# Normalizing half the rows ahead of the other half's additions at the ends of two graph layers

## The chip, the core and the metric

The kernel runs on one core of one Trainium2 chip. The metric is the time of one execution in device microseconds; the time before is the median of 6 runs. A core has five engines with a queue of instructions each: PE (TensorE, matrix products; its weight loads are listed apart as PEld), DVE (VectorE), ACT (ScalarE), POOL (GpSimd) and SP (SyncE, which here issues transfers). Each engine takes its instructions strictly in the order in which they were built; a wait for another engine holds everything behind it on the same engine. Products land in PSUM and are copied out by DVE or ACT (an evacuation); everything else lies in SBUF, 128 partitions wide, or in DRAM.

## The reference

Four graph layers run one after the other on 2708 nodes with 128 features and one dense adjacency matrix `adj`, each followed by a residual addition and a layer norm:

```
x = layernorm(x + L0(x, adj))   # messages gelu(s_i + d_j + b), summed with weights adj_ij; update with gelu, inner layernorm
x = layernorm(x + L1(x, adj))   # gated messages, see below; update with relu, inner layernorm
x = layernorm(x + L2(x, adj))   # a hyperbolic layer over all pairs
x = layernorm(x + L3(x, adj))   # two rounds of adj @ x with swish
```

Layer 1, whose start and end the change touches:

```
messages = x @ W_msg + b_msg
logits = (messages @ W_q) @ (messages @ W_k).T / sqrt(128) + gate_bias
gates = sigmoid(logits) * adj * adj
updated = relu(concat([x, gates @ messages]) @ W_upd + b_upd)
out = (updated - mean) / sqrt(var + eps) * gamma + beta
```

So at the end of layers 0 and 1 each row is normalized twice: first the layer's own result `h`, which is scaled by gamma and added to x + beta, and then the sum. The second result is the x of the next layer.

## The kernel before, in words

**Tiles.** x is held as 22 tiles of 128 rows (the last has 20). `groups()` gives groups of 4 tiles, `runs()` two halves: tiles 0 to 10 (early) and 11 to 21 (late).

**The two normalizations.** `moments` (L197) takes one bn_stats per tile on DVE. `normalize` (L199 to L230) works out the scale `r` and the offset `off` of every row of a half in some ten small DVE instructions of 128x11 (L129, L150, L205) with one square root on ACT between them (L145), and then shifts each tile: even tiles on DVE (L230), odd ones on ACT (L228). `Resnorm.add(a, b)` normalizes `h`, multiplies it by gamma (L241), adds it to `xb`, which is x + beta (L242), and takes the moments of the sum. `Resnorm.end(a, b)` normalizes x itself. `Resnorm.all` runs add of the early half, add of the late half, end of the early half, end of the late half.

**End of layer 0.** It is written in the order in which it shall run (`manual_schedule`). `U.sums(n)` forms the update of a group on PE (L821), adds it on DVE (L822) and applies Gelu on ACT (L823); `U.rows(n)` adds x (L828), takes moments and adds beta to x on POOL (L830). After five groups `U.norm.add` runs for the early half; then come the sums and rows of the last two tiles, then the late half and both ends. After that stand the five small DVE instructions of the bad count (L899 to L904; a count of rows for which the sparse method of layer 0 would not hold), a 1x1 product on PE (L906), and a copy of it to `bad_n` (L907), which is read before layer 3.

**Start of layer 1.** A scheduler places these instructions by their operands. PE turns W_q and W_k (L1007), multiplies them to `w_qk` (L1012); then, for each group, x is turned (L1019) and copied to `xT` on ACT (L1020), `ps_m` (L1022) gives the messages, copied to mT on ACT (L1023), `ps_q` (L1025) the queries, copied to qT on DVE (L1026), and `ps_w` (L1031) gives messages and the x part of the update side by side, which DVE copies to `both` with a bias (L1032). For that, POOL first copies two weights and two biases into `w_both` and `b_both` (L1001, L1002). POOL also forms `xb` (L1034). In the main loop `lg` (L1063), a sigmoid (L1064), two multiplications by the adjacency tile (L1065, L1066) and `acc` (L1070) run for each tile; SyncE loads the adjacency tiles (L1054) into three buffers.

**End of layer 1 and start of layer 2.** `norm.all()` closes layer 1, in written order. Then, placed by the scheduler: x is turned (L259), copied to another `xT` on DVE and ACT in turn (L261), multiplied by the layer 2 weights (L1176), copied to `M` on ACT (L1177), and DVE takes its moments (L1179) before a long chain of small instructions.

Of the kernel before, what the change touches and what calls it, by code (L numbers as in the profile page):

```python
# [12 lines left out]
F32 = mybir.dt.float32  # L13
# [3 lines left out]
ALU = mybir.AluOpType  # L17
# [3 lines left out]
P = 128  # L21
BANK = 512
# [12 lines left out]
def spans(start, stop, step):  # L35
    return [(a, min(a + step, stop)) for a in range(start, stop, step)]
# [3 lines left out]
def gnn_stack(ctx: ExitStack, tc: tile.TileContext, t, out: bass.AP):  # L40
    nc = tc.nc
    N, D = t["x"].shape
# [6 lines left out]
    const = ctx.enter_context(tc.tile_pool(name="const", bufs=1))  # L49
# [5 lines left out]
    @functools.cache  # L55
    def weight(name, k0=0):
        w = const.tile([P, D], F32, name=f"w_{name}_{k0}")
        nc.sync.dma_start(out=w, in_=t[name][k0:k0 + P, :])
        return w

    @functools.cache
    def column(name):
        c = const.tile([P, 1], F32, name=f"col_{name}")
        nc.sync.dma_start(out=c, in_=t[name].rearrange("(p o) -> p o", o=1))
        return c

    @functools.cache
    def across(name):
        n = t[name].shape[0]
        r = const.tile([P, n], F32, name=f"row_{name}")  # L70
        nc.gpsimd.dma_start(out=r, in_=t[name].partition_broadcast(P))
        return r


    x = keep.tile([P, NT, D], F32, name="x")
    xsq = keep.tile([P, NT], F32, name="xsq")
    bad_n = keep.tile([1, 1], mybir.dt.int32, name="bad_n")
# [13 lines left out]
    def over_tiles(r, n=NT, p=P):  # L91
        return r[:p, None, :].to_broadcast([p, n, r.shape[1]])
# [8 lines left out]
    class Values:  # L101
# [33 lines left out]
        def add(self, a, b):  # L135
            return self.tt(a, b, ALU.add)
# [53 lines left out]
    def runs(n=2):  # L190

        return [(NT * k // n, NT * (k + 1) // n) for k in range(n)]

    def moments(st, src, a, b):

        for i in range(a, b):
            nc.vector.bn_stats(out=st[:, i, :], in_=src[:, i, :])  # L197

    def normalize(dst, src, st, a, b, V, sq=None):  # L199

        even, odd, m2, m5 = (st[:, a:b, k] for k in (1, 4, 2, 5))

        def stt(in0, scalar, in1, op0, op1):
            o = V.new(in0)
            nc.vector.scalar_tensor_tensor(o, in0, scalar, in1, op0=op0, op1=op1)  # L205
            return o


        d = V.tt(even, odd, ALU.subtract)
        q = stt(d, 1.0 / 16.0, d, ALU.mult, ALU.mult)  # L210
        if sq is None:
            m = stt(m2, LN_EPS * D, m5, ALU.add, ALU.add)
            w = stt(m, 0.25 / D, q, ALU.mult, ALU.add)
        else:
            m = V.tt(m2, m5, ALU.add)
            var = stt(m, 0.25 / D, q, ALU.mult, ALU.add)
            w = V.ts(var, 0.25 * LN_EPS, ALU.add)

        root = V.act(w, AF.Sqrt)
        both = V.tt(even, odd, ALU.add)  # L220
        r = V.recip(V.add(root, V.mul(w, V.recip(root))))
        off = stt(both, -0.5, r, ALU.mult, ALU.mult)
        if sq is not None:
            nc.vector.scalar_tensor_tensor(sq[:, a:b], var, 4.0 * D, V.mul(r, r), op0=ALU.mult, op1=ALU.mult)
        for i in range(a, b):
            c = slice(i - a, i - a + 1)
            if i % 2:
                nc.scalar.activation(dst[:, i, :], src[:, i, :], AF.Identity, bias=off[:, c], scale=r[:, c])  # L228
            else:
                nc.vector.tensor_scalar(dst[:, i, :], src[:, i, :], r[:, c], off[:, c], op0=ALU.mult, op1=ALU.add)  # L230

    class Resnorm:


        def __init__(self, h, xb, g, st, st2, V, sq=None):
            self.h, self.xb, self.g, self.st, self.st2, self.V, self.sq = h, xb, g, st, st2, V, sq

        def add(self, a, b):
            h = self.h
            normalize(h, h, self.st, a, b, self.V)  # L240
            nc.vector.tensor_tensor(h[:, a:b, :], h[:, a:b, :], over_tiles(self.g, b - a), op=ALU.mult)  # L241
            nc.vector.tensor_tensor(x[:, a:b, :], self.xb[:, a:b, :], h[:, a:b, :], op=ALU.add)  # L242
            moments(self.st2, x, a, b)

        def end(self, a, b):
            normalize(x, x, self.st2, a, b, self.V, self.sq)

        def all(self):
            for a, b in runs():
                self.add(a, b)  # L250
            for a, b in runs():
                self.end(a, b)

    def transposed(dst, src, psum):

# [121 lines left out]
    with ExitStack() as l0:  # L377
        wp = l0.enter_context(tc.tile_pool(name="l0", bufs=1))
        aggT = wp.tile([P, LT * LR], F32, name="aggT")
        msg_s, msg_d = weight("L0_msg_wT", 0), weight("L0_msg_wT", P)  # L380
        upd_x, upd_a = weight("L0_upd_wT", 0), weight("L0_upd_wT", P)
        msg_b, msg_br = column("L0_gnn_msg_b"), across("L0_gnn_msg_b")
        upd_b, ln_w, ln_b = across("L0_gnn_upd_b"), across("L0_gnn_ln_w"), across("L0_gnn_ln_b")
# [4 lines left out]
        with ExitStack() as msg:  # L388
# [37 lines left out]
            with tc.tile_pool(name="pre0", bufs=1) as pp:  # L426
# [3 lines left out]
                    out=trif[:, :JB], in_=trif[:, :JB], compare_op=ALU.is_gt, fill=0.0, base=0,  # L430
# [23 lines left out]
            p_misc = msg.enter_context(tc.tile_pool(name="ps_misc", bufs=1, space=PSUM))  # L454
# [378 lines left out]
            U = Update()  # L833
# [4 lines left out]
            with tc.manual_schedule():  # L838
# [43 lines left out]
                for step in last_turn:  # L882
                    step()
                U.rows(ahead - 1)
                early, late = runs()
                U.norm.add(*early)
                for n in range(ahead, G):
                    U.sums(n)
                for n in range(ahead, G):
                    U.rows(n)  # L890
                U.norm.add(*late)
                U.norm.end(*early)
                U.norm.end(*late)


                most = vp.tile([P, 1], F32, name="most")
                ones = vp.tile([P, 1], F32, name="ones")
# [4 lines left out]
                nc.vector.tensor_tensor(bad, bad, fine, op=ALU.subtract)  # L902
                nc.vector.tensor_scalar(bad, bad, 1.0, None, op0=ALU.add)
                nc.vector.tensor_reduce(most, bad, AX.X, ALU.add)  # L904
                ps = p_misc.tile([P, BANK // P, P], F32, name="ps")
                nc.tensor.matmul(ps[:1, 0, :1], ones, most, start=True, stop=True)  # L906
                nc.vector.tensor_copy(bad_n, ps[:1, 0, :1])  # L907

    def all_pairs():

# [65 lines left out]
    def layers_1_to_3(top, before_end=lambda: None):  # L976

        with ExitStack() as l1:
# [6 lines left out]

            both = wp.tile([P, NT, 2 * D], F32, name="both")
            mrow, h = both[:, :, :D], both[:, :, D:]
            w_both = wp.tile([P, 2 * D], F32, name="w_both")
            b_both = wp.tile([P, 2 * D], F32, name="b_both")
            xb = wp.tile([P, NT, D], F32, name="xb")  # L990
            w_msg, w_q, w_k = weight("L1_gnn_W_msg"), weight("L1_gnn_W_q"), weight("L1_gnn_W_k")
            upd_x, upd_a = weight("L1_gnn_W_upd", 0), weight("L1_gnn_W_upd", P)
            msg_bc, msg_br = column("L1_gnn_b_msg"), across("L1_gnn_b_msg")
            gate_b = across("L1_gnn_gate_bias")
            upd_b, gamma, beta = across("L1_gnn_b_upd"), across("L1_gnn_ln_gamma"), across("L1_gnn_ln_beta")

            with ExitStack() as pre:
                psum = pre.enter_context(tc.tile_pool(name="ps_pre1", bufs=2, space=PSUM))
                nc.gpsimd.memset(both[:, NT - 1, :], 0.0)
                for k, (w, b) in enumerate(((w_msg, msg_br), (upd_x, upd_b))):  # L1000
                    nc.gpsimd.tensor_copy(w_both[:, k * D:(k + 1) * D], w)  # L1001
                    nc.gpsimd.tensor_copy(b_both[:, k * D:(k + 1) * D], b)  # L1002

                wT = []
                for w in (w_q, w_k):
# [120 lines left out]
        with ExitStack() as l2:  # L1126
            wp = small
# [565 lines left out]
```

## Time and profile before

| what | value |
|---|---|
| median of 6 runs | 1961.28 us (1960.13 to 1963.07) |
| profiled execution | 1956.19 us |
| its span, first to last instruction | 1954.5 us |
| mean granted clock of TensorE | 0.924 |
| busy share of the span: PE, DVE, ACT, POOL | 84%, 79%, 57%, 35% |
| end of layer 0, from the last far sums' stage to the bad count's product | 879 to 927 us |
| start of layer 1 up to the first gate product | 927 to 954.89 us |
| end of layer 1 and start of layer 2 | 1172 to 1208 us |

Start times are us from the span's start. A group or a piece of the chain is named by engine, what is written, and line. "busy, mean" of an instruction is its own time; the step to a dependent instruction behind it is a little longer, and independent instructions of DVE overlap a little. The chain that ended last is followed back from the last instruction: at each step to what released it, or to the instruction before it on its engine. Queue waits (SPq) tell what a queue's next transfer waited for.

### The profile page before, as it was taken

To read this page: it belongs to the slowest core of one execution; us is meant where nothing else is said; L and a number is where in the kernel's file an instruction comes from. 1 tells how busy PE (TensorE), PEld (TensorE's weight loads), DVE (VectorE), ACT (ScalarE), POOL (GpSimd) and SP (SyncE) were. 2 spreads that over 40 slices of the span, in tenths; PEclk is the share of its full clock that TensorE was granted. 3 is DMA by queue.
4 is the path that set the end of the run, shared out by engine and by line. 5 is a ranking of instruction groups with operands and counts; after the bars stand their busy time and mean duration, and the time that the engine had idled before them with its cause. 6 is when DMAs were issued, how large, how long until landed. Compare 5 with 4: busy or idle time off the path is not lost.

```text
span 1954.5 us, 36493 instructions
## 1 busy us (share of the span) xinstructions
PE 1650.5 (84%) x13993; PEld 945.9 (48%) x13993; DVE 1549.0 (79%) x3657; ACT 1118.9 (57%) x1551; POOL 677.1 (35%) x431
## 2 busy tenths in 40 slices
PE   5999999999999999881999992899889972099995
PEld 4666666666666666661544441322223321044542
DVE  7899999999999999868688858699999997800104
ACT  3666676676676666653344434799989973300003
POOL 5677667667767767571100000020000440000000
PEclk9899999999999999995999996789999986599997
DMA  8756656666666566440344401122223207044320
GB/s 224 156 118 144 140 124 146 131 130 147 127 131 150 122 136 141 81 89 5 138 150 165 151 2 59 45 89 88 74 69 101 92 2 299 0 166 151 138 94 30
DMA packets 218695, 222.25 MB, mean 114 GB/s; under 512 B 28373, under 2 KB 204859, under 8 KB 212051
## 3 DMA queue, kind: packets, MB, share of 16 engines
q1 hardware_dynamic: 167470, 196.15, 32.5%
q0 software_dynamic: 51040, 23.68, 10.3%
q8 instruction: 111, 1.82, 0.4%
q14 instruction: 74, 0.60, 0.1%
HBM read 211.94 MB, written 7.83 MB: 112 GB/s over the span
## 4 chain that ended last, share of the span: by engine, by line
DVE 42%; PE 30%; POOL 8%; issue 7%; ACT 6%; DMA 6%; SPq 0%; DVEq 0%; ACTq 0%; POOLq 0%
PE acc L1604 10%; POOL far L739 7%; PE lg L1063 5%; PE acc L1070 5%; DVE ix L735 5%; DMA far<-d_tab,ix 4%; DVE W L840 3%; DVE w L1336 3%; DVE u L1322 3%; DVE m L1325 3%; DVE extra L753 2%; DVE o L697 2%; DVE S L665 2%; DVE m L1342 2%; PE sl L775 2%
## 5 line engine op out<-in xcount | busy, mean ns | idle before, releaser
L739 POOL DMA_INDIRECT far<-d_tab,ix x352 | 561.1, 1594 | 259.9 <-DVE W L840 112.5
L853 ACT ACTIVATE g<-sl 128x768 f32<-128x768 f32 x484 | 392.9, 812 | 257.9 <-PE sl L780 204.8
L775 PE MATMUL sl<-dA,S 124*128 124x153 f16 x4840 | 408.0, 231 | 10.4 <-DVE W L840 7.6
L775 PEld LDWEIGHTS <-S 124*128 124x128 f16 x4840 | 330.3, 98 | 79.9 <-issue 68.1
L791 PE MATMUL acc<-g,W 128*32 128x128 f32 x4840 | 205.5, 277 | 0.5 <-DVE W L840 0.5
L1296 POOL TENSOR_TENSOR at<-at,off 128x128 f32<-128x128 f32 (+1 forms) x22 | 69.4, 3167 | 337.6 <-DMA at<-in_adjT 322.4
L1604 PE MATMUL acc<-held,x 128*128 128x512 f32 (+1 forms) x240 | 99.7, 564 | 82.6 <-ACT x L228 82.6
L791 PEld LDWEIGHTS acc<-g,W 128*32 128x32 f32 x4840 | 140.6, 109 | 58.7 <-issue 54.8
L780 PE MATMUL sl<-s,same 50*128 50x384 f16 x968 | 161.8, 308 | 0.0
L280 DVE TENSOR_TENSOR g<-ps,row_L_gnn_b 128x512 f32<-128x512 f32 (+2 forms) x14 | 7.9, 573 | 191.7 <-PE ps L278 191.6
L1352 PE MATMUL accV<-m,X 128*128 128x512 f32 (+4 forms) x264 | 128.3, 628 | 33.8 <-DVE m L1342 29.4
L840 DVE TENSOR_TENSOR W<-sl,own 128x150 f32<-128x150 f32 x484 | 143.0, 299 | 14.8 <-ACT g L853 12.1
L1304 PE MATMUL ps<-XT 128*128 128x512 f32 (+4 forms) x264 | 143.1, 626 | 3.1 <-ACT m L1309 2.8
L1064 ACT ACTIVATE w<-lg,row_L_gnn_gate_bias 128x512 f32<-128x512 f32 (+1 forms) x132 | 83.4, 636 | 106.1 <-PE lg L1063 104.9
L665 DVE TENSOR_SCALAR S<-rk 124x1000 f16<-124x1000 bf16 (+1 forms) x330 | 132.8, 428 | 0.0
L735 DVE FIND_INDEX8 ix<-v,o 128x8 uint32<-128x2728 f32 x44 | 131.7, 2993 | 0.0
L1063 PE MATMUL lg<-qT,mT 128*128 128x512 f32 (+2 forms) x264 | 121.1, 547 | 3.6 <-ACT w L1064 3.1
L1070 PE MATMUL acc<-w,both 128*128 128x512 f32 (+2 forms) x264 | 121.2, 546 | 0.0
L753 DVE SCALAR_TENSOR_TENSOR extra<-far,v,extra 128x128 f32<-128x128 f32 x330 | 114.7, 348 | 6.3
L1604 PE MATMUL acc<-at,x 128*128 128x512 f32 (+3 forms) x288 | 118.4, 559 | 0.0
L697 DVE SCALAR_TENSOR_TENSOR o<-ps,ar 128x496 f32<-128x496 f32 x132 | 82.4, 624 | 37.5 <-issue 24.5
L1604 PEld LDWEIGHTS acc<-held,x 128*128 128x128 f32 x240 | 45.1, 197 | 134.8 <-ACT x L228 82.8
(315 smaller groups left out, 2618.8 us busy)
## 6 DMA issues: line engine op xcount, KB each, us to landing
at<-in_adjT SPq DMA_DIRECT2D x40, 1354.0 KB
ar<-in_adj SPq DMA_DIRECT2D x105, 248.0 KB
far<-s_tab SPq DMA_DIRECT2D x44, 512.0 KB
at<-in_adjT SPq DMA_DIRECT2D x42, 448.0 KB
at<-in_adjT SPq DMA_DIRECT2D x21, 704.0 KB
at<-in_adjT SPq DMA_DIRECT2D x21, 650.0 KB
held<-in_adjT SPq DMA_DIRECT2D x10, 1354.0 KB
at<-in_adjT SPq DMA_DIRECT2D x21, 280.0 KB
```

The lines of the kernel that those rows point to most:

```text
L665: nc.vector.tensor_scalar(self.S[h][:, :n, :, k * RG:(k + 1) * RG], self.rk[h][:, :n, :LR].rearrange("p b (c i) -> p b c i", c=NC), EDGE + ...
L735: nc.vector.max_index(ix, self.v[:, n * 8:n * 8 + 8], self.o.rearrange("p b j -> p (b j)"))
L739: nc.gpsimd.indirect_dma_start(out=self.far[n][:, k, :], out_offset=None, in_=d_tab[:, :], in_offset=bass.IndirectOffsetOnAxis(ap=self.ix[ ...
L753: nc.vector.scalar_tensor_tensor(self.extra, f, w, self.extra, op0=ALU.mult, op1=ALU.add)
L775: nc.tensor.matmul(group[c], self.S[h][:, n, c, :], dA[q][:, b, c, :], start=c % 3 == 0 and q == 0, stop=False)
L780: nc.tensor.matmul(out, same[p], self.s3[p, :e - a, :], start=False, stop=True)
L791: nc.tensor.matmul(self.acc[q:q + 32, k, :], W[:, c, :], g[:, c, :], start=b == 0 and k == 0, stop=ends)
L840: nc.vector.tensor_tensor(W[:, :, :RG].rearrange("p (k c) i -> p k c i", k=2), columns_of(sl, D, DA), own[:, None, None, :].to_broadcast([ ...
L853: nc.scalar.activation(g.rearrange("p (k c) d -> p k c d", k=2), columns_of(sl, 0, D), AF.Gelu, scale=1.0 / D_SCALE)
L1063: nc.tensor.matmul(lg, mT[:, j * P:j * P + r], qT[:, a:b], start=True, stop=True)
L1070: nc.tensor.matmul(acc[k], mrow[:rows[j], j, :], ws[j][:rows[j], a:b], start=j == 0, stop=j == NT - 1)
L1604: nc.tensor.matmul(acc[k], src[:rows[j], j, :], at[:rows[j], a:b], start=j == order[0], stop=j == order[-1])
```

## The change

`normalize` is split into `normalizer` (the row scales and offsets) and `shift` (their use), and `shift` is told which engine takes which tile. `Resnorm.begin` shifts a half of `h`, all eleven tiles on ACT; `add` no longer normalizes and works in pieces of up to 4 tiles; `end` takes a pattern of engines. The new order of `all` is: begin and add of the early half, whatever is given as `between`, begin of the late half, end of the early half with all shifts on DVE, add of the late half, end of the late half on both engines in turn. Layer 0 uses `all`, with the last two tiles' sums and rows and the count's product and copy as `between`; the count's five DVE instructions move ahead of it. `w_both` and `b_both` of layer 1 are loaded from DRAM side by side, where before the parts were loaded each to a tile of its own and copied together by POOL. The arithmetic on each value is the same.

```diff
+    @functools.cache
+    def side_by_side():
+        w = const.tile([P, 2 * D], F32, name="w_both")
+        r = const.tile([P, 2 * D], F32, name="b_both")
+        for k, (a, b) in enumerate((("L1_gnn_W_msg", "L1_gnn_b_msg"), ("L1_gnn_W_upd", "L1_gnn_b_upd"))):
+            nc.sync.dma_start(out=w[:, k * D:(k + 1) * D], in_=t[a][:P, :])
+            nc.gpsimd.dma_start(out=r[:, k * D:(k + 1) * D], in_=t[b].partition_broadcast(P))
+        return w, r
...
-    def normalize(dst, src, st, a, b, V, sq=None):
+    def normalizer(st, a, b, V, sq=None):
...
+        return r, off
+
+    def shift(dst, src, a, b, by, turns="va"):
+        r, off = by
         for i in range(a, b):
             c = slice(i - a, i - a + 1)
-            if i % 2:
+            if turns[i % len(turns)] == "a":
                 nc.scalar.activation(dst[:, i, :], src[:, i, :], AF.Identity, bias=off[:, c], scale=r[:, c])
             else:
                 nc.vector.tensor_scalar(dst[:, i, :], src[:, i, :], r[:, c], off[:, c], op0=ALU.mult, op1=ALU.add)
 
+    def normalize(dst, src, st, a, b, V, sq=None):
+        shift(dst, src, a, b, normalizer(st, a, b, V, sq))
...
+        def begin(self, a, b):
+            shift(self.h, self.h, a, b, normalizer(self.st, a, b, self.V), "a")
+
         def add(self, a, b):
-            h = self.h
-            normalize(h, h, self.st, a, b, self.V)
-            nc.vector.tensor_tensor(h[:, a:b, :], h[:, a:b, :], over_tiles(self.g, b - a), op=ALU.mult)
-            nc.vector.tensor_tensor(x[:, a:b, :], self.xb[:, a:b, :], h[:, a:b, :], op=ALU.add)
-            moments(self.st2, x, a, b)
-
-        def end(self, a, b):
-            normalize(x, x, self.st2, a, b, self.V, self.sq)
-
-        def all(self):
-            for a, b in runs():
-                self.add(a, b)
-            for a, b in runs():
-                self.end(a, b)
+            for k, m in spans(a, b, 4):
+                h = self.h[:, k:m, :]
+                nc.vector.tensor_tensor(h, h, over_tiles(self.g, m - k), op=ALU.mult)
+                nc.vector.tensor_tensor(x[:, k:m, :], self.xb[:, k:m, :], h, op=ALU.add)
+                moments(self.st2, x, k, m)
+
+        def end(self, a, b, turns="va"):
+            shift(x, x, a, b, normalizer(self.st2, a, b, self.V, self.sq), turns)
+
+        def all(self, between=lambda: None):
+            early, late = runs()
+            self.begin(*early)
+            self.add(*early)
+            between()
+            self.begin(*late)
+            self.end(*early, "v")
+            self.add(*late)
+            self.end(*late)
...
                 U.rows(ahead - 1)
-                early, late = runs()
-                U.norm.add(*early)
-                for n in range(ahead, G):
-                    U.sums(n)
-                for n in range(ahead, G):
-                    U.rows(n)
-                U.norm.add(*late)
-                U.norm.end(*early)
-                U.norm.end(*late)
...
-                ps = p_misc.tile([P, BANK // P, P], F32, name="ps")
-                nc.tensor.matmul(ps[:1, 0, :1], ones, most, start=True, stop=True)
-                nc.vector.tensor_copy(bad_n, ps[:1, 0, :1])
+
+                def between():
+                    ps = p_misc.tile([P, BANK // P, P], F32, name="ps")
+                    nc.tensor.matmul(ps[:1, 0, :1], ones, most, start=True, stop=True)
+                    for n in range(ahead, G):
+                        U.sums(n)
+                    nc.vector.tensor_copy(bad_n, ps[:1, 0, :1])
+                    for n in range(ahead, G):
+                        U.rows(n)
+
+                U.norm.all(between)
...
-            w_both = wp.tile([P, 2 * D], F32, name="w_both")
-            b_both = wp.tile([P, 2 * D], F32, name="b_both")
...
+            w_both, b_both = side_by_side()
+            w_msg, w_q, w_k = w_both[:, :D], weight("L1_gnn_W_q"), weight("L1_gnn_W_k")
+            upd_a, msg_bc = weight("L1_gnn_W_upd", P), column("L1_gnn_b_msg")
...
-                for k, (w, b) in enumerate(((w_msg, msg_br), (upd_x, upd_b))):
-                    nc.gpsimd.tensor_copy(w_both[:, k * D:(k + 1) * D], w)
-                    nc.gpsimd.tensor_copy(b_both[:, k * D:(k + 1) * D], b)
```

## The prediction

> **What bounds the kernel now.** I read the page's busy shares first: no engine bounds the whole span, so the change is worth what its stages are worth.
>
> ```profile
> span 1954.5 us, 36493 instructions
> ...
> PE 1650.5 (84%) x13993; PEld 945.9 (48%) x13993; DVE 1549.0 (79%) x3657; ACT 1118.9 (57%) x1551; POOL 677.1 (35%) x431
> ```
>
> Then a table by stage (start:end, length, busy time of PE, weight loads, DVE, ACT and POOL, granted clock, DMA share, GB/s). The diff touches the end of layer 0 with the start of layer 1 (first two rows) and the end of layer 1 (third). In the first and third DVE works nearly all the time, PE hardly, and the clock is low.
>
> ```profile
> 879.00:927.20 48.20, 8.55 (x66) 7.13 (x58) 40.38 (x138) 19.07 (x42) 8.69 (x8) 0.58 0.02 3
> 927.20:955.00 27.80, 26.05 (x101) 16.68 (x102) 12.50 (x23) 7.25 (x14) 7.36 (x6) 0.93 0.37 150
> 1172.00:1208.30 36.30, 10.24 (x66) 9.40 (x66) 32.24 (x132) 15.99 (x41) 1.16 (x5) 0.62 0.11 38
> ```
>
> Third, the chain that ended last, over those stretches (start, length, work). It runs through every part of the normalization, then through the bad count (L907), the weight turn (L1007) and layer 1's products:
>
> ```profile
> 899.30 2.04 ACT o L228 x5
> 901.36 1.64 DVE o L241
> 903.09 1.64 DVE x L242
> 904.75 2.22 DVE g L197 x11
> ...
> 911.10 2.42 ACT o L228 x6
> ...
> 927.48 0.15 DVE bad_n L907
> ...
> 929.55 1.71 PE ps L1019 x8
> ...
> 939.75 1.13 PE ps_m L1022 x2
> ```
>
> and at layer 1's end:
>
> ```profile
> 1185.02 2.42 ACT both L228 x6
> ...
> 1196.68 2.61 PE ps L259 x11
> ...
> 1204.65 3.68 DVE st L1179 x19
> ```
>
> So a microsecond here is a microsecond of the end. Fourth, SyncE's queue: layer 1's first adjacency load waits for the count, because its buffer lies over the count's temporaries.
>
> ```profile
> SPq L1054 <- DVE most L904: 69.5, 1, 69.5
> ```
>
> Last, the granted clock (before the DMA share) around an idle spell of PE: 1.00 while PE finishes at about 884, half some 3 us later.
>
> ```profile
> 884.00:886.00 2.00, 0.34 (x4) 0.15 (x2) 1.97 (x7) 0.89 (x2) 1.19 (x2) 1.00 0.00 0
> 886.00:888.00 2.00, 0.00 (x0) 0.00 (x0) 1.86 (x5) 0.00 (x0) 0.49 (x1) 0.71 0.00 0
> 888.00:890.00 2.00, 0.50 (x2) 0.53 (x3) 1.89 (x6) 0.02 (x1) 0.00 (x0) 0.50 0.00 0
> ```
>
> **The change, part by part.** I follow the changed program's queues as built, with durations from these rows.
>
> *Prices.* A shift of one tile costs ACT 0.405 us (five in 2.03) and DVE 0.272 (six in 1.63). Before, the multiply, addition and moments of 11 tiles took 5.53 (901.36 to 906.89). In pieces of 4, 4 and 3 a 128x512 addition takes 0.71 to what depends on it (882.31 to 883.02), four moments 0.79 (883.02 to 883.81): 2.21 per piece of 4. The piece of 3 is scaled from that: 0.58 + 0.58 + 0.59 = 1.75. Together 6.17, 0.64 more per half. An independent DVE instruction of 128x512 steps in 0.60 (881.70 to 882.31).
>
> *End of layer 0.* Step 1: the count's five small DVE instructions (926.07 to 927.10, 1.03) now stand ahead of the early normalizer, which starts at 896.46 for 895.43; its 3.87 (a table load in it) end at 900.33. Step 2: DVE needs only the first four of ACT's eleven shifts (1.62), 901.98; additions 6.17, 908.15. Step 3: the last two tiles took 2.04 (906.89 to 908.93). Into this comes bad_n, the wait for PE to turn W_q (0.57, from 927.62 to 928.19), two copies (0.51) and w_qk (0.29), while a wait for Gelu and meetings with POOL of about 0.5 go: 3.05, so 911.2. Step 4: late normalizer 2.1 (2.17 in layer 0, 2.06 in layer 1): 913.3. Step 5, a new wait: ACT has all eleven late shifts queued (4.45, until 917.75) ahead of the root for the early rows' second normalization. DVE is ready for the root at 914.0 and stands 3.8 us; behind it are the eleven early shifts and all late additions. From root to first shift 1.38 (919.77 to 921.15), eleven shifts on DVE 2.99: early rows done at 922.15. Step 6: late additions 6.17, among them now three `both` and two qT of layer 1's first eight tiles, 5 x 0.60, less 0.4 of dependent gaps that they fill: 930.9. One more `both` and the normalizer (0.60 + 2.07): 933.5. Six shifts on ACT 2.42, xT's copy 0.64 (939.11 to 939.75): the product ps_m of tiles 8 to 11 starts at 936.6. Before it started at 939.75, the same work behind it. Gain 3.1. If the inserted evacuations cost no time the gain is 5.7, if each costs its full 0.69 and the waits around W_q come out twice as long it is about 1.5. I take 3.1, as the rows used are of the same instructions.
>
> *Clock there.* PE idles from about 930.4 to 933.7, just the length of the idle spell shown above. Two passes of 512 took 2.04 at half clock (L1304 at 1224.47, granted 0.50) and 1.12 at full clock: 0.92 a product. Bounds 0 (clock holds) and 1.5; I take 0.5, because the first products after the gap would be cold and their evacuations have slack.
>
> The Trainium skill ("TensorE: Matmul & The Clock Gate", section "Why this matters for your kernels") says that TensorE should not idle for more than about 3 us between bursts, or it falls back to half clock, and this speaks against splitting the rows: each half's turn is a small burst with a gap behind it. The trace's fall at about 3 us of idling agrees; by the rule the clock would surely be lost in this gap, and the sum below would be 1 us higher.
>
> *Removed copies, earlier loads.* The four POOL copies of weights and biases (927.51 to 928.50) go; they lay beside the turn of W_q and W_k (to 929.34), were first needed at 932.08, and would cost 1.0 without that cover. The same number of DMAs goes through SyncE's and POOL's queues at the start, two in other places, hundreds of us before their use: 0. SyncE's three adjacency loads start at about 897, not 927. Their data was in by 940 (DMA share 0 from 940 to 948.5) and is first used at 958.10, so no one waits less: 0. The next load waits for a buffer, as before. POOL's xb (6.14) starts when the last x is done, as before, beside DVE work that reads PSUM.
>
> *End of layer 1.* Same steps, no count. Early normalizer unchanged, off at 1175.3; four shifts 1176.98 (before, eleven on two engines ended at 1177.39); additions 6.17: 1183.18 (before 1182.96). Late normalizer 2.06: 1185.24. ACT's eleven shifts to 1189.7; the early rows' root is behind them, DVE ready at 1186.2, a wait of 3.5. Root to shift 1.55, eleven shifts 2.99: 1194.23. Late additions 6.17: 1200.4, where before both halves were summed at 1192.93. What was gained for it? Little: xT's copies stand behind these additions, one on DVE, the other on ACT waiting for the last addition, as xT lies over xb. The last normalizer takes 3.35 (1192.93 to 1196.28, V0T's memset in it) and now also a copy of xT (0.60) and three moments (0.35 in the gaps): 1204.7. Its shifts began at 1200.74 and ended at 1203.44 on ACT; now they end at 1207.0: 3.5 later. The ten products and M's last copies behind that are the same (1203.44 to 1208.25), one copy less. Loss 3.5; 2.5 if that copy and the moments shorten the tail by 1, 4.5 if the interleaved moments cost their whole 0.2 each and the copy of M holds the shifts. PE's part is at half clock for the early products (12 passes in 2.38, against 20 in 2.61): 0.3, between 0 and 1.
>
> **Sum:** -3.1 + 0.5 + 3.5 + 0.3 = +1.2 us. The profiled execution took 1956.19 (span 1954.5 and 1.7 around it), which gives 1957.4; the median of the runs, 1961.28, lies 5.09 higher, so 1962.5.
>
> **Rivals.** *Additions behind cold products (slower).* DVE's queue is in order, and in step 6 the late additions now stand behind `both` and qT, which wait for PE, just woken at half clock at about 919. A group of four tiles has two products of 0.92 more each when cold and 0.86 for ps_w, 2.7; two groups 5.4, of which DVE's own work covers about half: 2.5 more, and 1 for the later gap. That is -3.1 + 0.5 + 3.5 + 3.8 = +4.7: 1966. For it: PE was at 0.50 until 931 after its 927 start. Against: `both` and qT come 2 to 4 us after their operands by my count. It decides from 2.7 us of DVE waiting for ps_w and ps_q. *Overlap worth more (faster).* The evacuations hide wholly (gain 5.7) and layer 1 loses only 2.0, as half its M work is ahead: -3.7, with the clock kept -4: 1957.3. For it: DVE has gaps between dependent small instructions. Against: DVE is the engine with 40.38 busy of 48.20. *Loads collide.* The three early loads run at 897 to 908 beside the additions; a tenth on 10 us of DVE is +1.0 on my sum: 1963.5. Against: the same loads ran at 927 to 940 beside PE with matmuls at their usual length. *Nothing happens* (the early rows are not ahead at all) is excluded for the order of the queues, but in layer 1 it is nearly my forecast: ahead, and unused.
>
> **How the numbers follow.** Even, my forecast: 0.63, 1962.5, own range 1959.5 to 1965. Cold products 0.23, 1966. More overlap 0.10, 1957.3. Collision 0.04, 1963.5. 0.2% is 3.9 us, about what a measurement tells from no change: the first and last lie within it, so same 0.67, slower 0.23, faster 0.10. The terms at their ends sum to -3.2 (-5.7 + 2.5) and +5.5 (-1.5 + 1.5 + 4.5 + 1), so 1958.1 to 1966.8; the range of 1957 to 1967 takes these in, reaches to both rivals' centres and leaves out their far halves.
>
> **What would show it.** Right: a wait of DVE for ACT's root of 3 to 4 us in both layers (before 0.2); the count's product on PE at about 897; layer 1's first ps_m near 922; ps_m of tiles 8 to 11 near 936.6 and the first gates' product near 952 to 953 instead of 954.89; `st<-M` (before until 1208.33) ending near 1209.5, since layer 1 starts 2.6 earlier and its end takes 3.8 longer. Wrong: no root wait; DVE waiting for ps_w or ps_q by more than 2.7 us; layer 1's main loop of another length than 204.5; a change in the pair stage or layer 3, which the change does not touch.

## The result: no difference that can be told, and the profile after

The changed kernel takes 1961.48 us (median of 32 runs, 1959.80 to 1963.38) against 1960.88 of the kernel before (68 runs, 1957.13 to 1963.16). The ratio is 1.0004, with a 95% interval of 0.9999 to 1.0009: between 0.2 us less and 1.8 us more. The forecast was 1.2 us more.

For what follows I cut both profiles at marks that both have: the start of the last four moments ahead of layer 0's first normalizer (894.64 before, 897.41 after), the first gates' product `lg`, the end of layer 1's last moments of h, and the end of the last moments of `M`. Here are those stretches of the kernel after, and below them layer 0's end and layer 1's end of the kernel before (start:end, length, busy time of PE, weight loads, DVE, ACT and POOL, granted clock, DMA share, GB/s).

```profile
897.41:956.43 59.02, 31.42 (x105) 18.93 (x105) 37.79 (x129) 23.31 (x51) 8.60 (x5) 0.69 0.18 71
956.43:1174.85 218.42, 212.64 (x575) 96.44 (x575) 172.87 (x314) 95.09 (x151) 0.00 (x0) 1.00 0.32 117
1174.85:1213.34 38.49, 12.36 (x66) 9.97 (x66) 30.55 (x127) 16.91 (x45) 1.23 (x5) 0.60 0.09 34
1213.34:1960.00 746.66, 589.86 (x1658) 233.14 (x1658) 490.31 (x810) 410.76 (x452) 70.06 (x22) 0.86 0.27 96
```

```profile
894.64:954.89 60.25, 25.94 (x100) 16.57 (x100) 39.67 (x127) 21.35 (x45) 9.52 (x9) 0.70 0.17 69
...
1173.32:1208.33 35.01, 10.24 (x66) 9.40 (x66) 30.95 (x126) 14.69 (x39) 1.16 (x5) 0.61 0.11 40
```

Between the same marks the kernel before took 60.25, 218.43, 35.01 and 746.17. So layer 0's end ("stretch A" from here on) gained 1.2 us, layer 1's end ("stretch B") lost 3.5, the main loop between them is the same to a hundredth, and the rest differs by 0.5. The 2.8 by which the first mark lies later is not the change's: in the fourteen profiles of this study it lies between 894.6 and 897.5, and the earliest is that of the kernel before.

The end of layer 0, from the timeline of the kernel after (start, duration, what, and in brackets the idle time of the engine before it with what ended it). To compare with times of the kernel before, take 2.77 off.

```profile
916.30 4.34 ACT L244 ACTIVATE o<-o,g 128x128 f32<-128x128 f32 x11 [1.17 <-DVE g L216]
...
920.54 0.20 ACT L155 ACTIVATE g<-g 128x11 f32<-128x11 f32 x1
920.77 0.23 DVE L160 RECIPROCAL g<-g 128x11 f32<-128x11 f32 x1 [3.84 <-ACT g L155]
...
921.91 2.91 DVE L246 TENSOR_SCALAR x<-x,g 128x128 f32<-128x128 f32 x11
922.31 2.27 PE L1038 MATMUL ps<-ident,x 128*128 128x128 f32 x8 [8.66 <-DVE x L246]
...
924.73 0.69 DVE L263 TENSOR_TENSOR o<-o,row_L_gnn_ln_w 128x512 f32<-128x512 f32 x1
...
936.79 1.40 PE L1038 MATMUL ps<-ident,x 128*128 128x128 f32 x5 [3.67 <-DVE x L246]
...
939.29 2.07 PE L1041 MATMUL ps_m<-xT,w_both 128*128 128x512 f32 x2 [1.10 <-ACT xT L1039]
```

The eleven late shifts hold ACT from 916.30 to 920.54; only then comes the root of the early rows' second normalizer, and DVE has stood 3.84 us for it. Behind it are DVE's eleven early shifts, and behind those all the late additions. The products of the early rows begin at 922.31, those of tiles 8 to 11 at 936.79 after a gap of 3.67 on PE, and `ps_m` there takes 2.07, where before it took 1.13. The granted clock explains that (same columns as above, the clock is third from the end):

```profile
934.00:936.00 2.00, 0.00 (x0) 0.00 (x0) 1.67 (x9) 0.21 (x1) 0.00 (x0) 1.00 0.00 0
936.00:938.00 2.00, 1.21 (x5) 0.79 (x5) 1.60 (x7) 1.64 (x5) 0.00 (x0) 0.72 0.00 0
938.00:940.00 2.00, 0.90 (x2) 0.50 (x2) 0.00 (x0) 1.72 (x5) 1.15 (x1) 0.50 0.00 0
...
942.00:944.00 2.00, 2.00 (x5) 1.20 (x4) 0.69 (x1) 0.09 (x1) 2.00 (x1) 0.57 0.00 0
```

It falls to half at about 936.9 and is back at about 943.7. From the start of `ps_m` of tiles 8 to 11 to the first `lg` are 17.14 us; before, for the same work, 15.14.

At the end of layer 1 the same wait stands, from the timeline of the kernel after:

```profile
1186.93 4.34 ACT L244 ACTIVATE both<-both,v,v 128x128 f32<-128x128 f32 x11 [1.17 <-DVE v L216]
1191.18 0.19 ACT L155 ACTIVATE v<-v 128x11 f32<-128x11 f32 x1
1201.35 0.58 ACT L287 COPY xT<-ps 128x512 f32<-128x512 f32 x1 [9.98 <-issue]
```

```profile
1191.41 0.23 DVE L160 RECIPROCAL v<-v 128x11 f32<-128x11 f32 x1 [3.64 <-ACT v L155]
...
1192.71 2.90 DVE L246 TENSOR_SCALAR x<-x,v,v 128x128 f32<-128x128 f32 x11
```

DVE stands 3.64 us. The early rows are shifted by 1195.6, but ACT's copy of their `xT` comes at 1201.35, after the last addition: ahead and unused.

### The profile page after: what moved, and what is told of

The parts are those of the page before. It is cut to its first block, busy times and chain, and to the rows that moved or that the text cites. A ratio compares the mean times of both kernels' runs of the same rounds, so it can differ in the third digit from the quotient of the medians.

```text
span 1960.0 us, 36503 instructions
## 1 busy us (share of the span) xinstructions
PE 1665.2 (85%) x13993; PEld 953.0 (49%) x13993; DVE 1546.8 (79%) x3661; ACT 1123.0 (57%) x1563; POOL 677.9 (35%) x427
```

## The experiments

All ratios are against the kernel before on the same chip, with a 95% interval; stretches A and B are from one profile each. Some of the expectations measure a stretch between other marks, so their lengths do not all compare with A and B (36.2 and 39.6 stand there for B's 35.0 and 38.5); their differences do.

**The change again, and each layer alone.** First whether the stretches belong to the kernel or to one execution, and whether the two layers add up. The second run undoes layer 1, the third layer 0:

```diff
+        def in_turn(self, between=lambda: None):      # the order of the kernel before
+            early, late = runs()
+            for n, (a, b) in enumerate((early, late)):
+                if n:
+                    between()
+                h = self.h[:, a:b, :]
+                normalize(self.h, self.h, self.st, a, b, self.V)
+                nc.vector.tensor_tensor(h, h, over_tiles(self.g, b - a), op=ALU.mult)
+                nc.vector.tensor_tensor(x[:, a:b, :], self.xb[:, a:b, :], h, op=ALU.add)
+                moments(self.st2, x, a, b)
+            for a, b in (early, late):
+                self.end(a, b)
...
-                    norm.all()              # layer 1, in the second run
+                    norm.in_turn()
...
-                U.norm.all(between)         # layer 0, in the third run, with the count behind it again
+                U.norm.in_turn(between)
```

> The changed kernel once more, for a second profile of it: if its stretches are its own and not those of one execution, layer 0's end takes 59.0 again (with ps_m of tiles 8 to 11 at half clock, 2.07) and the stretch from the first gates' product to the last moments of M 253.4, against 60.3 to 61.0 and 249.7 in the old order; the ratio is within 0.9995 and 1.0012. Rival: a part of these was the state of the clock in one execution; the first would then differ by over 0.7 or the second by over 0.5.

> Changed kernel with layer 1's normalization put back to the order of the kernel before (both halves' additions first, shifts on two engines, additions in one piece); layer 0 stays as changed. Theory 'two layers that nearly cancel': layer 0's end gains 1.3 us and layer 1's end costs 3.5 by the two profiles, so this kernel takes 1.3 less than the kernel before (about 1959.6 against 1960.9) and the stretch from layer 1's last moments to layer 2's first instruction is 36.2 again. Rival 'layer 1 is not the loss': the 3.5 of the one profile is not a property of the order, the stretch stays near 39.6 and the time near the changed kernel's 1961.5.

> Changed kernel with layer 0's end put back to the order of the kernel before (the bad count after the normalization too); layer 1 stays as changed, the weights stay side by side from DRAM. Theory 'two layers that nearly cancel': 3.5 us more than the kernel before, about 1964.4, the stretch at layer 0's end back at 59.5 and the one at layer 1's end at 39.6, with DVE's wait for the root of 3.6 in layer 1 alone. Rival 'layer 0 gains nothing': if the gain of 1.3 in layer 0 is only the difference of two single profiles, this kernel takes the changed kernel's 1961.5.

| kernel | time, us | ratio | A | B |
|---|---|---|---|---|
| changed kernel, second measurement | 1962.09 | 1.0013 (1.0004 to 1.0022) | 60.34 | 38.49 |
| new order in layer 0 only | 1959.30 | 0.9991 (0.9982 to 1.0000) | 58.96 | 35.10 |
| new order in layer 1 only | 1963.99 | 1.0013 (1.0004 to 1.0022) | 61.01 | 38.55 |

The two layers do nearly cancel: about 1.8 less and 2.9 more, against 1.3 and 3.5 expected. Both rivals fall: B is 38.5 to 38.6 in every profile with layer 1 as in the changed kernel, and 34.8 to 35.3 in every profile with its old order. A is not so steady. The second profile of the same kernel has 60.34 and not 59.02, as its own expectation's rival had it, and its ratio lies just above the range expected; the three profiles with A as changed give 59.4 on average, the three with the old order (60.25, 61.01, and 60.83 below) 60.7. What varies is told in the last section. By the stretches the change costs 3.5 - 1.3 = 2.2; the two intervals of the whole time (0.9999 to 1.0009 and 1.0004 to 1.0022) meet at 0.8 to 1.8.

**The other parts.** The change also moves the bad count and takes four copies from POOL. Each was tried without the halves' new order (the first is the kernel before with `side_by_side` alone, the second the changed kernel with `in_turn` in both layers, the third the kernel before with the count alone), and then the halves' new order in layer 0 with the count left behind it.

```diff
 # the count's move alone, on the kernel before
+                nc.vector.tensor_reduce(most, bad, AX.X, ALU.add)      # and the four lines ahead of it
                 early, late = runs()
                 U.norm.add(*early)
+                ps = p_misc.tile([P, BANK // P, P], F32, name="ps")
+                nc.tensor.matmul(ps[:1, 0, :1], ones, most, start=True, stop=True)
                 for n in range(ahead, G):
                     U.sums(n)
+                nc.vector.tensor_copy(bad_n, ps[:1, 0, :1])
                 for n in range(ahead, G):
                     U.rows(n)
                 U.norm.add(*late)
                 U.norm.end(*early)
                 U.norm.end(*late)
```

> Kernel before with one part of the change alone: layer 1's weights and biases side by side from DRAM, without the four copies on POOL. Forecast of the prediction: 0, since the copies lay beside the turn of the weights; 1960.9 within 0.8, and the stretch at layer 0's end 59.5. Rival: the copies (1.0 in all) or the placement of the loads at the start do count, 1 us less or more, or the early loads make layer 0 itself longer or shorter.

> Only two parts of the change: weights side by side, and the bad count (with the turn of W_q and W_k, which stands behind it) moved up between the two halves of layer 0; the normalization itself stays in the old order in both layers. Theory 'the count is the gain': before, 2.0 us lie between the last shifted tile (927.2) and the first turn of x (929.34), filled by the count's product, its copy and the weights' turn; without them the turn of x starts 2.0 earlier, of which PE's half clock at its waking takes back up to 1.0. Then this kernel takes 1959.0 to 1960.0, the stretch at layer 0's end is 1 to 2 shorter than the 60.3 to 61.0 of the old order, and the halves' new order in layer 0 is worth nothing beside it. Rival 'the split is the gain': the count was hidden, this kernel takes 1960.9 and the stretch stays 60.3 to 61.0.

> Kernel before with the bad count alone moved up between the halves of layer 0; weights and biases are still set side by side by four copies on POOL. Theory 'the count alone': 5.5 below the kernel before, as with the weights from DRAM (about 1955.5). Rival 'the copies lose their cover': with the turn of x 3.5 earlier the copies of 1.0 on POOL stand in front of the first ps_w and cost up to 1.0, 1956.5; the stretch at layer 0's end is 56.5 and not 55.6.

> The new order of the halves in layer 0 without the count's move: the bad count and with it the turn of W_q and W_k stand behind the whole normalization, as in the kernel before; layer 1 in the old order, the weights side by side. Theory 'the count's move is the gain, the split in layer 0 a loss': the early rows are ready 4 earlier and PE cannot use them; DVE's wait for the root of 3.8 and the longer additions remain, so the turn of x starts 3.5 to 4 later than in the old order, the stretch at layer 0's end is 64 to 65 against 60.3 to 61.0, and the time about 1965. Rival 'the split gains as well, and the two gains overlap': the stretch is under 60 and the time under 1961.

| layer 1 in the old order throughout | time, us | ratio | A |
|---|---|---|---|
| weights side by side alone | 1961.07 | 1.0002 (0.9993 to 1.0011) | 60.83 |
| count moved, with the weights | 1955.12 | 0.9972 (0.9961 to 0.9982) | 55.59 |
| count moved, without the weights | 1955.43 | 0.9972 (0.9960 to 0.9983) | 55.35 |
| halves' new order, count left behind | 1965.07 | 1.0023 (1.0013 to 1.0032) | 65.16 |
| halves' new order and count moved (from above) | 1959.30 | 0.9991 (0.9982 to 1.0000) | 58.96 |

This is where the gain and the loss are. The weights are worth nothing that can be told, also where the count no longer holds things up. The count's move alone is worth about 5.5 us, far above the 1 to 2 that I expected of it; the halves' new order in layer 0 costs about 4, with the count moved (1959.3 against 1955.1) or not (1965.1 against 1961.1). The queue waits of PE in layer 0's end tell why (what waited for what: us in total, times, longest). The kernel before has in them

```profile
PE ps L906 <- DVE most L904: 33.0, 1, 33.0
```

and on its timeline

```profile
921.15 1.63 DVE L230 TENSOR_SCALAR x<-x,g 128x128 f32<-128x128 f32 x6
...
927.25 0.19 PE L906 MATMUL ps<-most,ones 128*1 128x1 f32 x2 [33.00 <-DVE most L904]
...
929.34 1.91 PE L1019 MATMUL ps<-ident,x 128*128 128x128 f32 x8
```

whereas the kernel with only the count and the weights moved has

```profile
925.87 1.94 PE L1051 MATMUL ps<-ident,x 128*128 128x128 f32 x8 [13.20 <-DVE x L246]
```

Before, a 1x1 product stood at the head of PE's queue for 33 us and held the turns of the early rows, which are shifted from 921.15 on. They began at 929.34, 34.7 after the first mark. With the count out of the way they begin 28.9 after it (925.87 with the mark at 896.95): as soon as DVE has shifted them, while the late rows are still being normalized. The old order already had the early rows ready ahead of the late ones; nobody could use them. The adjacency loads, which also start earlier with the count, are no part of the gain: the main loop takes 218.42 to 218.44 in all fourteen profiles. My expectation of 1 to 2 counted from the last shifted tile (927.2), so it missed this too.

With the count left behind the new order, PE waits 37.0 us for it, from the profile of that kernel:

```profile
PE ps L943 <- DVE most L941: 37.0, 1, 37.0
```

**The roots ahead of the shifts.** The wait that the new order makes is taken away by issuing both small normalizers before the late shifts.

```diff
             self.add(*early)
             between()
-            self.begin(*late)
-            self.end(*early, "v")
+            first = normalizer(self.st, *late, self.V)
+            second = normalizer(self.st2, *early, self.V, self.sq)
+            shift(self.h, self.h, *late, first, "a")
+            shift(x, x, *early, second, "v")
             self.add(*late)
```

> Changed kernel with one difference: both small normalizers (the late rows' first, the early rows' second) are issued before the late rows' eleven shifts, so ACT computes the early root ahead of its shifts. Theory 'the root behind the shifts': DVE's waits for the root of 3.84 in layer 0 and 3.64 in layer 1 fall to about 0.3; ACT's shifts start 0.9 later, and DVE's eleven early shifts of 2.9 cover that. 3.5 less in layer 0 and 3.4 in layer 1, 6.9 less than the changed kernel, about 1954.6, faster than the kernel before by 0.3%. Rival 'the wait only moves': the late additions then wait for ACT's late shifts, or PE's waking from half clock sets layer 0's end; layer 0 gives under 1.5, and the time is 1957 to 1958. Rival 'layer 1 is bound by its split additions': layer 1's stretch stays above 38.

It takes 1955.90 us, ratio 0.9974 (0.9965 to 0.9983): by the medians 5.6 below the changed kernel (6.9 expected). B is 35.09, as in the old order: 3.4 of 3.4, so in layer 1 the wait makes up the whole loss (whatever else the new order costs and gains there comes out even), and the rival of the split additions falls. A is 56.41, 2.6 below the changed kernel's first profile and 3.0 below the mean, of 3.5. Where the rest went, from the timelines of DVE, ACT and PE of this kernel in layer 0:

```profile
916.63 0.23 DVE L160 RECIPROCAL g<-g 128x11 f32<-128x11 f32 x1 [0.19 <-ACT g L155]
...
920.73 1.04 ACT L1041 COPY xT<-ps 128x512 f32<-128x512 f32 x2
921.35 2.08 PE L1043 MATMUL ps_m<-xT,w_both 128*128 128x512 f32 x2 [0.91 <-ACT xT L1041]
...
925.17 0.69 DVE L1053 TENSOR_TENSOR both<-ps_w,b_both 128x512 f32<-128x512 f32 x1 [0.79 <-PE ps_w L1052]
...
930.25 0.69 DVE L1047 COPY qT<-ps_q 128x512 f32<-128x512 f32 x1 [0.90 <-PE ps_q L1046]
```

The root is there after 0.19. Now PE's first products are late, and the late additions stand behind `both` and `qT`, 1.7 us in all. The products are late for two reasons: they run at half clock (`ps_m` takes 2.08), and ACT, which has the late shifts until about 920.7, copies `xT` only 2.6 after the first turn (918.17), where in the changed kernel it was 1.4 (922.31 to 923.67). So the expectation's rival "the wait only moves" holds in part. In the changed kernel these waits come to 0 in the first profile and 0.9 in the second (0.41 and 0.52). That is the prediction's rival of the cold products, in a small size and below the 2.7 from which it was to decide; it grows once the first wait is gone. In layer 0 this kernel is still no better than the count's move alone (A 55.4 to 55.6). The 0.8 to 1.1 between them is about what half clock behind its second gap on PE costs: from `ps_m` of tiles 8 to 11 to the first `lg` are 16.4 (936.88 to 953.30) against 15.1.

**The clock in the gap.** Four products that nobody reads were put into PE's gap of 3.7 us in the changed kernel.

```diff
                                                 op=ALU.add)
+                    if a == BANK // D:
+                        for _ in range(4):
+                            ps = psum.tile([P, BANK], F32, name="ps_m")
+                            nc.tensor.matmul(ps, w_qk, mT[:, :BANK], start=True, stop=True)
```

> Changed kernel with four additional products of 128x512, whose results nobody reads, put on PE into the gap of 3.7 us ahead of the turn of x's tiles 8 to 11 in layer 0, so that the clock stays up. Theory 'half clock behind the gap costs 2': the two passes of ps_m of tiles 8 to 11 take 1.13 instead of 2.07, the stretch from that product to the first gates' product is 15.2 as in the old order instead of 17.1, and the time is 1.5 to 2 below the changed kernel's 1961.5. Rival 'it costs 0.5, as forecast': the stretch falls by 0.5 and the time is 1961. The four products may also hold up the turn of x by up to 0.5.

The timeline of PE in this kernel:

```profile
933.58 2.74 PE L1056 MATMUL ps_m<-mT,w_qk 128*128 128x512 f32 x6
...
939.39 1.12 PE L1041 MATMUL ps_m<-xT,w_both 128*128 128x512 f32 x2 [1.29 <-ACT xT L1039]
```

`ps_m` takes 1.12, and from it to the first `lg` are 15.15 us (939.39 to 954.54), just the 15.14 of the kernel before: the half clock behind the gap costs 2.0, not 0.5. What the products bring on the whole is less clear. The first of the four products landed ahead of the last early `ps_w` and held it up by 0.85, and `ps_m` started 42.96 after the first mark, where the two profiles of the changed kernel have 41.88 and 42.76; A is 58.11, between 0.9 and 2.2 below theirs, while the time, 1961.23 (1.0004, 0.9995 to 1.0013), shows no gain, with an interval too wide to exclude one of a microsecond. The price is shown, a remedy is not.

**The clock at layer 1's first turn.** The same idea in front of the first turn, on the better kernel (count moved, old order).

```diff
                 nc.vector.tensor_copy(w_qk, ps[:, :P])
+                for _ in range(20):          # 25 in the second
+                    ps = psum.tile([P, 2, 2 * D], F32, name="ps_w")
+                    nc.tensor.matmul(ps[:, 0, :], wT[1], w_both, start=True, stop=True)
```

> The kernel with the count moved and both layers in the old order, and twenty additional products of 128x256, whose results nobody reads, on PE in its 13 us of idling ahead of layer 1's first turn of x. Theory 'PE wakes at half clock on the path': with the clock up, the first eight turns take 1.0 instead of 1.94, the first ps_m 1.1 instead of 2.08 and the first eight ps_w 1.0 instead of 1.93; the stretch at layer 0's end falls from 55.6 to 53.1 to 54.0 and the time to about 1953. Rival 'other engines set it': copies on ACT and additions on DVE pace these products, the stretch falls by under 0.7 and the time stays at 1955.

> The same with twenty-five additional products instead of twenty: the twenty ended 3.15 us before the first turn of x, and the granted clock was back at 0.50 when that began, so that run did not test it. These end about 1 us before it. Theory 'PE wakes at half clock on the path': clock 1.00 from the first turn on, the eight turns take 1.0 and ps_m 1.1, the stretch at layer 0's end 53.1 to 54.0 against 55.4 to 55.6 of the two kernels with the count moved and no additional products, the time about 1953. Rival 'other engines set it': stretch 55 or more, time 1955.

They take 1953.48 (0.9965, 0.9952 to 0.9979) and 1954.97 (0.9969, 0.9958 to 0.9980), which the intervals do not part from 0.9972, and A is 56.85 and 56.32, longer by 0.7 to 1.5 than without. Neither tests the theory. With twenty, PE stood 3.15 ahead of the first turn and the clock was down when that began; with twenty-five it was up then and fell in the middle of the products, from the table by stretch:

```profile
925.00:926.00 1.00, 0.00 (x0) 0.00 (x0) 0.90 (x5) 0.34 (x1) 0.00 (x0) 1.00 0.00 0
...
928.00:929.00 1.00, 0.78 (x2) 0.42 (x3) 0.58 (x4) 0.75 (x3) 0.00 (x0) 0.81 0.00 0
929.00:930.00 1.00, 1.00 (x3) 0.48 (x2) 0.93 (x5) 0.03 (x1) 0.00 (x0) 0.50 0.00 0
```

Whether a warm PE would shorten that path stays open.

**Memory of its own for layer 2's xT.** On the kernel with both roots first, `xT` got memory that does not lie over layer 1's buffers.

```diff
+        of2 = top.enter_context(tc.tile_pool(name="of2", bufs=1, side="right"))
+        XT = of2.tile([P, N], F32, name="XT")
...
-            XT = ap2.tile([P, N], F32, name="XT")
...
-                xT = pp.tile([P, N], F32, name="xT")
+                xT = XT
...
-                kept[j] = held.tile([P, N], F32, name=f"held{j}")
+                kept[j] = XT if j == 0 else held.tile([P, N], F32, name=f"held{j}")
```

> The kernel with both roots first, and layer 2's transposed x in memory of its own instead of over layer 1's buffers (it takes the place of the pair stage's XT, which is needed later, and of the first held adjacency tile after that). Theory 'ahead and unused': the early rows' copies of xT and their products no longer wait for the last addition; the late part is rid of one copy on DVE (0.6), of three moments (0.4) and of the products at half clock (3.45 for 16 passes), and the stretch from layer 1's last moments to layer 2 falls by 1.0 to 1.5 from 43.5; the time is about 1954.6 against 1955.9. Rival 'the tail is the same': the tail behind the last shift sets the end whatever lies ahead, gain 0 to 0.3.

1956.92 us, 0.9979 (0.9970 to 0.9988), and B is 36.26 against 35.09: no gain, rather a loss of 1. ACT's timeline of this kernel:

```profile
1191.01 0.56 ACT L289 COPY XT<-ps 128x512 f32<-128x512 f32 x1
1197.32 0.88 ACT L1199 COPY M<-ps 128x393 f32<-128x393 f32 x2 [5.75 <-DVE x L264]
```

`xT` is indeed copied early, 6 us ahead of the last addition, and its products run; but the next step, the copy to `M`, waits 5.75 us for the last addition just as `xT` had. So "unused" holds one step further on, and the expected 1.0 to 1.5 was wrong for not following the early rows to the end. Why the tail became longer was not separated; the scheduler also placed the products of the last fourteen tiles in one piece, at the end of the last copies of `xT`.

## Why the prediction was right, and where it was not

Its time holds (1962.5 against 1961.48), and so does "no difference that can be told". By its steps:

- **The new wait for the root** (step 5, 3.8 and 3.5 us): 3.84 and 3.64, and 3.8 and 3.6 in the second profile. Right, and the run with the roots ahead of the shifts shows that it is what the new order costs in layer 1.
- **Layer 0 up to the products of tiles 8 to 11** (steps 1 to 6, 936.6): 936.5 on the time base of the kernel before, 937.4 in the second profile. The steps between agree as well: the count's product came at 897.05 (about 897 forecast), the root of step 5 at 917.77 (917.75), the early rows were done at 922.0 (922.15). The first `ps_m` was forecast near 922 and came at 921.6. The late additions' rows were of the right size: DVE stood for `ps_w` and `ps_q` there by 0 and 0.9 in the two profiles, not by 2.7, so the slower rival did not decide.
- **The clock in the gap** ("I take 0.5", bounds 0 and 1.5): this term failed. The same work behind that product took 17.1 to 17.6 us in the changed kernel's two profiles against 15.1 to 15.2 in the old order, and 15.15 with the clock held up: 1.9 to 2.4. Both bounds were too low, because I priced only a first product or two at half clock, while nearly seven microseconds passed until the clock was back (936.9 to 943.7). The first `lg` came at 953.7 on the old time base (955.0 in the second profile), not 952 to 953, and layer 0 gained 1.3 on average instead of 2.6.
- **Layer 1's end** (loss 3.5, and 0.3 for the clock): 3.48 in both profiles, so the 3.5 is right and the 0.3 did not come. "Ahead, and unused" is right. The last moments of `M` ended at 1210.6 on the old time base, not near 1209.5, because layer 0 had gained less.
- **Copies, placement of loads** (0): right, alone and with the count moved. The rival of colliding loads has nothing for it: the first multiply, addition and moments of four tiles took 2.31 us beside the loads in layer 0 (904.70 to 907.01; DMA share 0.99 from 904.70 to 911.14) and 2.31 at layer 1's end (1178.57 to 1180.88; DMA share 0.00).
- **The sum** (+1.2): by the stretches +2.2; by the times +0.6 and, measured again, about +2. That 1962.5 came within 1.0 of the time is in part luck: the median that it started from, 1961.28 of 6 runs, lay 0.4 above that of 68 runs, while the change was put 1.0 lower than its stretches give.

What the prediction did not see is that its gain of 3.1 in layer 0 was the difference of two large terms. Step 1 gave the count's move the 1.03 of its own instructions, and the quoted chain even ran through its product, but I never asked who stood behind that product on PE. The move alone is worth 5.5, and the halves' new order, to which I had put the gain, loses about 4 of it in layer 0 and 3.5 in layer 1. The steps were followed for the change as a whole, so their sum came out; a reader who asked what to keep of it would have been told the wrong half. The version to keep is the kernel before with the count moved: 1955.1 to 1955.4 us, 0.28% below it, the intervals reaching from 0.17 to 0.40%.

## What to carry to other kernels

Where a change has several parts, price each one alone on the old order as well: a total near zero can hide a good part and a bad one. For every instruction that waits long at the head of an in-order queue, ask what stands ready behind it; a 1x1 product whose result was first read at 1611.8, more than 600 us later, held up the next layer by 5. And if a half is to be brought forward, follow it to its last consumer, and keep the short step that it depends on ahead of long work on the same engine.

## What was not expected of the hardware

In these profiles the granted clock changes only on a grid of 3.41 us. In the changed kernel's profile it rises at 926.65, falls at 936.89 and rises at 943.71 (worked out from the mean clock in stretches of 0.5 us): 10.24 and 6.82, three and two times 3.41. The second profile has 928.20, 938.44 and 945.26, the kernel with twenty-five additional products falls at 928.62 and rises at 932.04, and of some forty changes read in this study the intervals within a profile are such multiples to a few hundredths. The grid's place differs from execution to execution, and with it what half clock costs: PE's first work behind its long idling at layer 0's end was followed by the rise after 3.9 us in the kernel before (927.25 to 931.19) and 4.9 in the one with the weights alone (930.03 to 934.97). The first `ps_m` took 1.17 in the one and 1.66 in the other, and A was 60.25 and 60.83. Behind the second gap, 2.97 us in both, the kernel with both roots first had half clock for 3.41 us and the one with memory of its own for `xT`, the same in layer 0, for 6.82: A 56.41 and 57.82. So the variation of A by up to 1.4 between profiles of the same order goes with the grid's place; that nothing else varies was not tested. The Trainium skill ("TensorE: Matmul & The Clock Gate", section "Part 1: The HAM clock gate (the "warmup" mystery)") states this: activity is judged in free-running windows of 4096 cycles at 1.2 GHz, 3413 ns. The runs here agree, and they add what it means for a forecast: a gap of 3.0 to 3.7 us on PE cost not the part of a product but one or two windows at half clock, and a difference of a microsecond between two single profiles may be the grid's place alone. Nor does the clock fall a fixed 3 us behind PE's last work, as the prediction read it: it fell 2.5 us behind it in the kernel before (884.34 to 886.82) and 3.8 in the changed kernel (933.12 to 936.89).

Turns of x did not keep the clock up by themselves in one case: in the kernel with twenty-five additional products PE was busy for 2.00 of the 3.41 us ahead of the fall at 928.62, 1.60 of it with turns. In the kernel with both roots first the clock stayed up at the grid's 933.03 behind no more work (busy for 1.79 of 3.42 us, mostly products, with at most 0.66 of turns). In the kernel before it rose at 931.19 behind 3.03 us of work, at most 2.44 of it turns. So turns seem to count, but for less than products; three windows show no more than that, and what share of a window is needed was not measured.
